# Issue order of the score products: a full key tile's heads 0 and 2 ahead of the half tile's heads 1 and 3

## The chip, the cores and the metric

The kernel runs on one core of one Trainium2 chip. A core has five engines with instruction queues of their own: TensorE (matrix products), VectorE, ScalarE, GpSimd and SyncE (here it issues most DMAs). They meet only through semaphores. TensorE writes its results to PSUM, which has eight banks of 128 partitions; the other data stands in SBUF. The metric is device time in microseconds, the median of several executions.

## The reference

The input x is 4 images of 256 channels, 64 x 64 pixels, in float32. Two attention layers follow each other, each behind a group normalization with 32 groups and with a residual:

```python
x = x + L0(gn(x))      # 8 heads of 32; q from 4096 pixels, k and v by a 2x2 convolution with stride 2
x = x + L1(gn(x))      # 8 heads of 32; attention within 4 areas of 1024 pixels

# L0
attn = softmax((q . (k + pos)) * hd ** -0.5);  out = attn . v
# L1
attn = softmax((q . k) * hd ** -0.5)
out = conv1x1(attn . v + depthwise_conv7x7(v), w_proj, b_proj)
```

In both layers every query meets 1024 keys, so the inner work is the same: for each image, head and query 1024 scores, their exponentials, the sum of these, and the sum of values weighted by them.

## The kernel before, in words

The eight blocks (two layers, four images) are cut into 16 units each: a chunk of 512 queries with one group of four heads (four heads of 32 channels fill the 128 partitions of q and k). A unit goes through its 1024 keys in 8 key tiles of 128, so there are 1024 steps in all, each a unit's key tile. A step's scores are 128 keys (partitions) by 4 heads x 512 queries: four PSUM banks.

PSUM has six banks for scores, as three pairs s0, s1 and s2, and two for everything else. So a step and a half are worked on at a time. A phase (one round of the main loop from L1157, PHASES = 683 in all) computes the scores of one full step and of one half of another step (256 of the 512 queries): three steps in two phases. This is `scores(f)` (L430). Its pair `a` takes heads 0 and 2 of the full step, `b` heads 1 and 3, and `c` the half step's four heads: bank `h // 2` of c, in the right half of the bank for heads 1 and 3, in the left half for heads 0 and 2. The pairs rotate:

```python
a, b, c = [ps_banks(n, "s") for n in ((0, 1, 2) if f % 2 == 0 else (0, 2, 1))]
```

so a stands where the last phase's a stood, c where its b stood, b where its c stood.

A product (`score_product`, L419) is taken for one head at a time, as two matmuls of 64 keys each: the keys' 32 channels are the stationary operand, the queries the moving one. Head h stands on partitions 32h to 32h+31 and so uses the array's rows 32h to 32h+31; the two matmuls of a head use the two halves of its columns. Products of different heads can thus run in the array side by side, but heads 1 and 3 of the half tile and heads 0 and 2 of the half tile write the same two banks of c. A semaphore keeps these apart: each of the half tile's four matmuls for heads 1 and 3 adds one to `in_bank`, and the first matmul for heads 0 and 2 waits for the count (`wait_op`, L454; the Tile framework is told of it with a fence, L455, and adds no semaphore of its own to the counting matmuls, L448).

Three exponentials on ScalarE empty the pairs, in the order a, b, c (`exp_full` L457 with its ACTIVATE on L464, `exp_half` L466 with L475). In a phase, TensorE is given, one after the other: the scores; what the planner puts in of side work (projections, convolution by banded matrices, normalization's statistics, the softmax sums of L508), none to four parts; and the weighted sums of values of the phase before (`weighted`, L479, matmuls on L489). VectorE adds up the exponentials (`add_up`, L494, L499). When a unit ends, its sums go through `divisors` and `divide` (L501, L513), partly by DMA.

Within the main loop the order of every engine is the order in which the program issues (`manual_schedule`, L1100). How much side work goes into a phase is decided while the program is built, by `supply`, `pressure` and `busy` (L214, L248, L279) from counts and due times; they don't look at the order within `scores`.

Of the kernel before, what the change touches and what calls it, by code (L numbers as in the profile page):

```python
# [60 lines left out]
def direct_path(  # L61
# [107 lines left out]
    def ps_banks(n, name):  # L169
        return psum.tile([P, 2, CH], FP, tag=f"s{n}", name=name, bufs=1)  # L170
# [232 lines left out]
    def acc_of(g):  # L403
        if g not in accs:
            accs[g] = pool.tile([P, 4, CH], FP, tag="acc", name="acc", bufs=2)
        return accs[g]

    def pair_of(h):
        return slice(2 * (h % 2), 2 * (h % 2) + 2)

    def acc_half(g, u):
        return acc_of(g).rearrange("p (l b) (u n) -> p u b l n", l=2, u=2)[:, u]

    def parts_of(f):

        full, half = (3 * f + 1) // 2, (3 * f // 2 + 1, 0) if f % 2 == 0 else (3 * f // 2, 1)
        return (full if full < last else None), (half if half[0] < last else None)

    def score_product(out, s, h, cols):  # L419
        g, j = divmod(s, NKT)  # L420
        rows, unit = slice(HD * h, HD * h + HD), units[g]
        return [
            T.matmul(  # L423
                out[n : n + WIDE], lhsT=unit[2]()[rows, unit[0], j * P + n : j * P + n + WIDE],
                rhs=unit[1]()[rows, cols], start=True, stop=True,
            )
            for n in range(0, P, WIDE)
        ]

    def scores(f):  # L430

        full, half = parts_of(f)
        a, b, c = [ps_banks(n, "s") for n in ((0, 1, 2) if f % 2 == 0 else (0, 2, 1))]
        every = slice(0, CH)

        def half_product(h):

            u = half[1]
            return score_product(
                c[:, h // 2, HC * (h % 2) : HC * (h % 2) + HC], half[0], h, slice(HC * u, HC * u + HC)  # L440
            )

        if half is not None:
            for h in (1, 3):
                for first in half_product(h):
                    first.then_inc(in_bank, 1)
                    tc.add_to_no_dep_group(f"first_{f}", first.ins)
                    tc.no_tile_sem_insts.add(first.ins.name)  # L448
                    bank_count[0] += 1
        for h in (0, 2, 1, 3):  # L450
            score_product((a, b)[h % 2][:, h // 2, :], full, h, every)
        if half is not None:
            second = [product for h in (0, 2) for product in half_product(h)]
            second[0].wait_op(in_bank, bank_count[0], "sem-ge")  # L454
            tc.declare_fence(second[0].ins, group=f"first_{f}")  # L455

        def exp_full(n):  # L457
            g, j = divmod(full, NKT)
            if j == 0:
                p = acc_of(g)[:, pair_of(n), :]  # L460
            else:
                p = pool.tile([P, 2, CH], FP, tag="p", name="p", bufs=PB)
            made_p[full, n] = p
            S.activation(p, (a, b)[n], AF.Exp, scale=SCALE)  # L464

        def exp_half():  # L466
            if half is None:
                return
            (g, j), u = divmod(half[0], NKT), half[1]
            if j == 0:  # L470
                p = acc_half(g, u)
            else:
                p = pool.tile([P, 2, CH], FP, tag="p", name="p", bufs=PB).rearrange("p b (l n) -> p b l n", l=2)
            made_p[half[0], 2 + u] = p
            S.activation(p, c.rearrange("p b (l n) -> p b l n", l=2), AF.Exp, scale=SCALE)  # L475

        return [lambda: exp_full(0), lambda: exp_full(1), exp_half]
# [679 lines left out]
    while f < PHASES or before or plan or side or quick or norms_left or to_add or to_divide:  # L1157
        now[0], phase[0] = step, f
        exps = scores(f) if f < PHASES else [lambda: None] * 3
        mine = []  # L1160
        if f < PHASES:
            full, half = parts_of(f)
# [667 lines left out]
```

## Time and profile before

| | |
|---|---|
| median of three runs | 3091.56 us (3090.89 to 3096.43) |
| the profiled execution | 3092.91 us, its span 3090.8 us |
| granted TensorE clock, mean | 0.996 |
| TensorE matmuls busy | 3036.6 us (98% of the span), 47254 instructions |
| TensorE weight loads busy | 1282.2 us (41%) |
| VectorE busy | 2516.2 us (81%) |
| ScalarE busy | 2455.2 us (79%) |
| GpSimd busy | 483.1 us (16%) |
| score matmuls (L423) | 10928 + 10912 matmuls, 543.5 + 537.8 us busy |
| weighted sums (L489, all forms) | 4784 + 4776 matmuls with p, 449.9 + 450.6 us busy |
| exponentials (L464, full tile) | 1194 + 172, 1025 and 1023 ns each |
| exponentials (L475, half tile) | 598 + 84, 1036 and 1045 ns each |

A group of instructions has a line, an engine, an operation, and the tiles that it writes and reads (out<-in). PE stands for TensorE's matmuls, PEld for its weight loads, ACT for ScalarE, DVE for VectorE, POOL for GpSimd, SPq for the queue of SyncE. A float32 matmul of the program stands in the trace as two weight loads and two matmuls, its two passes. A matmul's start is recorded; its end is modelled, and overlapping matmuls are merged in a busy time, so a TensorE that is busy 98% of the time may still stall between matmuls. In a timeline, a row begins with its start and its length in us, merges like instructions, and has in brackets how long the engine sat idle before it and what ended that wait. A row of the waits has who waited for whom, the total in us, how many times, and the longest.

### The profile page before, as it was taken

What the parts mean: (1) busy time and instruction counts of PE and PEld (TensorE: products, weight loads), DVE (VectorE), ACT (ScalarE), POOL (GpSimd) and SP (SyncE); (2) the same over time, 40 slices, a digit from 0 to 9 for tenths busy, and PEclk for the clock granted to TensorE, in tenths of its full rate; (3) what the DMA queues carried; (4) which work ended last, traced back from release to release, by engine and by line L of the source; (5) the groups of instructions that cost most, each with busy time, mean ns of one, the idle gap of its engine ahead of it and who ended that gap; (6) DMA issues with size and microseconds to landing.
All of it is one profiled execution on the core that took longest, in us unless ns stands there. A gap on an engine that the chain in (4) does not pass through costs nothing. (4 is left out here: it accounts for less than half of the span.)

```text
span 3090.8 us, 108514 instructions
## 1 busy us (share of the span) xinstructions
PE 3036.6 (98%) x47254; PEld 1282.2 (41%) x47254; DVE 2516.2 (81%) x2721; ACT 2455.2 (79%) x2988; POOL 483.1 (16%) x921
## 2 busy tenths in 40 slices
PE   9999999999999999999999999999999999999998
PEld 6444333444444444334444444443444444443332
DVE  3788977789887787777888888777888888888888
ACT  3888877888888888788888887777777787788885
POOL 0111111111211111111112111111111111111111
PEclk9999999999999999999999999999999999999999
DMA  5244433566334556777865667667655565542222
GB/s 189 60 100 116 98 80 76 112 147 155 92 99 135 143 151 143 183 184 197 207 171 149 162 172 196 165 170 181 174 153 144 150 163 148 150 106 75 54 68 65
DMA packets 648316, 423.61 MB, mean 137 GB/s; under 512 B 411772, under 2 KB 556636, under 8 KB 647832
## 3 DMA queue, kind: packets, MB, share of 16 engines
q1 hardware_dynamic: 619384, 380.11, 48.6%
q0 software_dynamic: 28448, 36.48, 4.7%
q8 instruction: 373, 6.11, 0.8%
q14 instruction: 111, 0.91, 0.1%
HBM read 318.32 MB, written 98.09 MB: 135 GB/s over the span
## 5 line engine op out<-in xcount | busy, mean ns | idle before, releaser
L499 DVE TENSOR_TENSOR acc<-acc,p 128x1024 f32<-128x1024 f32 x1790 | 2113.9, 1218 | 424.9 <-PE av L489 313.6
L464 ACT ACTIVATE p<-s 128x1024 f32<-128x1024 f32 x1194 | 1159.4, 1025 | 416.5 <-PE s L423 406.0
L475 ACT ACTIVATE p<-s 128x1024 f32<-128x1024 f32 x598 | 619.6, 1036 | 0.3 <-DVE acc L499 0.2
L423 PE MATMUL s<-q,k_A 32*64 32x256 f32 (+1 forms) x10928 | 543.5, 497 | 17.1 <-ACT p L464 16.2
L423 PE MATMUL s<-q,k_B 32*64 32x512 f32 (+1 forms) x10912 | 537.8, 494 | 2.8 <-ACT p L464 2.0
L489 PE MATMUL av<-p,v_B 128*32 128x512 f32 (+1 forms) x4776 | 450.6, 487 | 0.0
L489 PE MATMUL av<-p,v_A 128*32 128x256 f32 (+1 forms) x4784 | 449.9, 486 | 0.0
L423 PEld LDWEIGHTS s<-q,k_A 32*64 32x64 f32 x10928 | 266.3, 131 | 342.6 <-ACT p L464 73.3
L423 PEld LDWEIGHTS s<-q,k_B 32*64 32x64 f32 x10912 | 267.2, 130 | 325.6 <-PE s L423 60.8
L534 POOL DMA_DIRECT2D rb<-recs x508 | 252.0, 502 | 526.7 <-DMA recs<-few 441.1
L532 POOL DMA_DIRECT2D recs<-few x127 | 70.0, 551 | 1407.6 <-DVE sums L531 1248.3
L489 PEld LDWEIGHTS av<-p,v_B 128*32 128x32 f32 x4776 | 149.3, 110 | 264.1 <-issue 238.2
L489 PEld LDWEIGHTS av<-p,v_A 128*32 128x32 f32 x4784 | 149.0, 110 | 228.9 <-issue 187.2
L464 ACT ACTIVATE acc<-s 128x1024 f32<-128x1024 f32 x172 | 167.0, 1023 | 82.1 <-PE s L423 81.9
L508 PE MATMUL den<-acc,ones 128*32 128x512 f32 x1024 | 140.8, 608 | 5.1 <-DVE acc L499 4.3
L524 POOL DMA_DIRECT2D few<-rows x127 | 71.2, 561 | 458.0 <-DMA rows<-den_sb 452.9
L167 PE MATMUL ops<-cv,wp_sb 128*32 128x512 f32 x1024 | 125.1, 598 | 6.1 <-DVE xm L828 3.2
L167 PE MATMUL k1ps<-h,wqkv_sb 128*32 128x512 f32 x1024 | 123.8, 598 | 2.7 <-ACT k_B L730 2.0
L167 PE MATMUL q0ps<-hq,wq_sb 128*32 128x512 f32 x1024 | 124.0, 598 | 1.4 <-ACT q L661 1.4
L167 PE MATMUL q1ps<-h,wqkv_sb 128*32 128x512 f32 x1024 | 124.3, 598 | 0.0
L167 PE MATMUL vals_ps<-hv,wqkv_sb 128*32 128x512 f32 x1024 | 124.1, 598 | 0.0
L167 PE MATMUL v0ps<-wkv,taps 128*32 128x256 f32 x2048 | 124.0, 386 | 0.0
(103 smaller groups left out, 2150.3 us busy)
## 6 DMA issues: line engine op xcount, KB each, us to landing
rows<-vals SPq DMA_DIRECT2D x384, 195.9 KB
rb<-recs POOLq DMA_DIRECT2D x508, 64.0 KB, 3.3
share<-vals SPq DMA_DIRECT2D x128, 195.9 KB
vala<-vout SPq DMA_DIRECT2D x128, 144.0 KB
vals<-vout SPq DMA_DIRECT2D x128, 144.0 KB
vc<-vala SPq DMA_DIRECT2D x64, 288.0 KB
band<-mats SPq DMA_DIRECT2D x96, 176.0 KB
hq<-in_x SPq DMA_DIRECT2D x32, 512.0 KB
```

The source lines that it names most:

```text
L167: T.matmul(out[cols, :], lhsT=lhsT[:, cols], rhs=rhs, start=start, stop=stop)
L423: T.matmul(out[n : n + WIDE], lhsT=unit[2]()[rows, unit[0], j * P + n : j * P + n + WIDE], rhs=unit[1]()[rows, cols], start=True, stop=True,)
L464: S.activation(p, (a, b)[n], AF.Exp, scale=SCALE)
L475: S.activation(p, c.rearrange("p b (l n) -> p b l n", l=2), AF.Exp, scale=SCALE)
L489: T.matmul(out, lhsT=v[:, j, unit[0] * P + HD * h : unit[0] * P + HD * h + HD], rhs=rhs, start=(j == 0 and not u), stop=(j == NKT - 1), sk ...
L499: V.tensor_add(to, to, p)
L508: T.matmul(dens[g][HD * h : HD * h + HD, :], lhsT=ones, rhs=p(h), start=(n == 0), stop=(n == len(sets) - 1),)
L524: G.dma_start(few[:, 0, :], rows.rearrange("h (q n) -> (h q) n", n=CH // HD))
L532: G.dma_start(recs.rearrange("h (q n) -> (h q) n", n=CH // HD), few[:, 1, :])
L534: G.dma_start(rb[HD * h : HD * h + HD, :], recs[h : h + 1, :].to_broadcast([HD, CH]))
```

## The change

In `scores`, the four matmuls of the full tile's heads 0 and 2 (pair a) are issued ahead of the four of the half tile's heads 1 and 3 (pair c). The full tile's heads 1 and 3 (pair b) and the half tile's heads 0 and 2 (pair c) follow as before. The number of instructions, their shapes, the banks, the counts on `in_bank` and the wait for them are the same.

```diff
@@ -440,6 +440,8 @@
                 c[:, h // 2, HC * (h % 2) : HC * (h % 2) + HC], half[0], h, slice(HC * u, HC * u + HC)
             )
 
+        for h in (0, 2):
+            score_product(a[:, h // 2, :], full, h, every)
         if half is not None:
             for h in (1, 3):
                 for first in half_product(h):
@@ -447,8 +449,8 @@
                     tc.add_to_no_dep_group(f"first_{f}", first.ins)
                     tc.no_tile_sem_insts.add(first.ins.name)
                     bank_count[0] += 1
-        for h in (0, 2, 1, 3):
-            score_product((a, b)[h % 2][:, h // 2, :], full, h, every)
+        for h in (1, 3):
+            score_product(b[:, h // 2, :], full, h, every)
         if half is not None:
             second = [product for h in (0, 2) for product in half_product(h)]
             second[0].wait_op(in_bank, bank_count[0], "sem-ge")
```

## The prediction

> **Names.** A phase is one call of scores(f). Its sixteen score products come in four groups of four (two heads, two 64-key column tiles each): H, the half tile's heads 1 and 3 (256 wide, array rows 32-63 and 96-127); A, the full tile's heads 0 and 2 (512 wide, rows 0-31 and 64-95); B, the full tile's heads 1 and 3 (512, same rows as H); C, the half tile's heads 0 and 2 (256, same rows as A). Before: H, A, B, C. After: A, H, B, C. The trace has two passes (two weight loads and two matmuls) for each product, written H1, H2 and so on.
>
> **What bounds the kernel now.** I read the page first, then all waits, then the timeline of single phases. From the page:
>
> ```profile
> span 3090.8 us, 108514 instructions
> PE 3036.6 (98%) x47254; PEld 1282.2 (41%) x47254; DVE 2516.2 (81%) x2721; ACT 2455.2 (79%) x2988; POOL 483.1 (16%) x921
> ```
>
> TensorE has 98%, VectorE and ScalarE about 80%. A busy TensorE may still be stalled inside, so the waits decide (engine and line, who is waited for: total us, times, longest):
>
> ```profile
> ACT p L464 <- PE s L423: 406.0, 506, 2.8
> ...
> PEld s L423 <- PE s L423: 119.1, 631, 0.2
> ...
> PE s L423 <- ACT p L464: 18.2, 23, 5.9
> ```
>
> ScalarE's exponential waits for TensorE 506 times; TensorE's score matmuls wait for ScalarE 23 times. TensorE is the bound. The middle line is a weight load of scores that waits for scores: the fence on in_bank ahead of C, in 631 phases, 0.19 us each. The timeline of a common phase shows where it lies:
>
> ```profile
> 1507.40 0.64 PEld L423 LDWEIGHTS s<-q,k_A 32*64 32x64 f32 x24 [0.41 <-ACT q L661]
> 1507.40 1.55 PE L423 MATMUL s<-q,k_A 32*64 32x256 f32 x32
> ...
> 1508.23 0.27 PEld L423 LDWEIGHTS s<-q,k_A 32*64 32x64 f32 x8 [0.19 <-PE s L423]
> ...
> 1508.59 1.02 ACT L464 ACTIVATE p<-s 128x1024 f32<-128x1024 f32 x1 [0.58 <-PE s L423]
> 1508.88 0.16 PEld L489 LDWEIGHTS av<-p,v_A 128*32 128x32 f32 x8 [0.38 <-issue]
> 1508.88 0.64 PE L489 MATMUL av<-p,v_A 128*32 128x256 f32 x8
> ```
>
> The last eight weight loads (C) come 0.83 us after the head, the next work 1.48 us after it. Record by record, from the first matmul: H1 0, A1 0.027, H2 0.267, B1 0.483, A2 0.507, B2 0.912, C1 0.936, C2 1.152. A 256-wide pass takes 0.216, a 512-wide one 0.429 (start to start); a first pass after its load costs 0.051 more. Rows of H and B end at 0.932+0.429 = 1.361, rows of A and C at 1.172+0.216 = 1.388; 0.088 later the next work starts, at 1.476. 616 of the 680 phases that can be compared have 1.476 within 0.004: the beat is fixed by the array, and the C load at 0.826 is early enough for its slot at 0.936.
>
> The exceptions are 52 phases in which B's bank is late (it waits for the third exponential of the phase before), as here:
>
> ```profile
> 3057.91 0.24 PEld L423 LDWEIGHTS s<-q,k_B 32*64 32x64 f32 x16 [1.11 <-ACT p L464]
> 3057.91 2.00 PE L423 MATMUL s<-q,k_B 32*64 32x256 f32 x32 [0.20 <-ACT p L464]
> ...
> 3058.82 0.24 PEld L423 LDWEIGHTS s<-q,k_B 32*64 32x64 f32 x16 [0.68 <-ACT p L475]
> ...
> 3059.84 0.16 PEld L489 LDWEIGHTS av<-p,v_B 128*32 128x32 f32 x8 [0.78 <-issue]
> ```
>
> There the next work starts 1.93 us after the head. A fresh group loaded at 0.91 costs the phase 0.46.
>
> **What the Trainium skill says.** "TensorE: Matmul & The Clock Gate", section "The cost: per-tile semaphore tail": matmuls that run side by side complete in program order, and their semaphore increments are serialized, about 26 ns each. The trace's semaphore updates agree on the order and not on the size. In a common phase H's four counts stand at 0.655, 0.698, 0.740 and 0.783 (0.0425 apart), A's update at 1.158, B's at 1.563, C's at 1.656. In the late phase that starts at 2812.505, C's last pass starts at 1.235, before B's last at 1.418, yet C's update comes at 2.142, 0.093 after B's 2.049, just as in the common phase: it is held until the earlier product has been reported. The same page's "The mechanism" has starts in strict order as well; this trace does not (C2 before B2 there). "TensorEngine Tiling (Array Packing)", "Key Properties", has a drain at each change of tiling: 0.092 at the head, 0.088 at the end. Its "Gotcha 1: PSUM Pressure" forbids two row tiles in one bank at once, which is what the fence is for; no run here shows it broken.
>
> **The change, part by part.** All time from the first matmul of the phase.
>
> 1. Removed: the head's wait for the second exponential of the phase before; A needs only the first. 28 phases with late B waited at the head for 7.4 us in all (0.27 each). Added: H has a wait of its own. Satisfied, it costs nothing: phase 5 already has a satisfied wait on the fifth load of its first batch, and the loads stay 7 ns apart. TensorE has 598 more waits of that kind. VectorE, GpSimd and SyncE have the same instruction order, ScalarE too; no DMA moves past anything.
>
> 2. Array time: unchanged. A1 0, A2 0.480, slot of C 0.909; H1 0.027, H2 0.293, B1 0.509, B2 0.938, end 0.958+0.429+0.088 = 1.475 against 1.476. The two row pairs swap roles.
>
> 3. The first exponential: the last phase, which has no half tile, issues its 512-wide group first. Its update is at 1.131 instead of 1.158. In a common phase ScalarE starts 0.027 earlier; it waits for TensorE anyway, so worth nothing.
>
> 4. The fence. H's matmuls now stand behind A in program order, and H carries the counts on in_bank that C waits for. If completion is reported in program order, they cannot come before A's 1.131, though H is through at 0.53. Four counts of 0.0425 each: 1.174 to 1.301; a load follows the fourth by 0.0425 (0.783 to 0.826 before): C1 is loaded at 1.344 instead of 0.826, and its slot of 0.909 is lost. From load to second pass 0.267, last of four 0.020, stream 0.216, drain 0.088: next work at 1.344+0.591 = 1.935. Against 1.476 that is 0.459 us per phase. Rows of A and C idle for 0.44. Behind C in TensorE's queue stand side work and the weighted sums, and nothing hides the gap, since TensorE is the bound: 682 phases have a fence, 682 x 0.459 = 313.0 us. What is late next is the whole following phase; ScalarE, DMA and VectorE gain slack.
>
> 5. Stalls that this absorbs. In the 52 late phases B's lateness (24.0 us beyond the beat) lies beside the new gap: each exponential of the phase before now comes about 0.49 earlier against the beat, so B starts near 0.70 and ends by 1.63, before C's 1.85. Less 24.0, and less the 7.4 of their heads. Some 39 us of other waits (15 at long heads, 9 at the ends of other score blocks, 15 among side work, mostly for DMA or ScalarE) get more time to pass; I take 16 of them as gone, bounds 0 and 39.
>
> Sum against the profiled execution's own 3092.9: 3092.9 + 313.0 - 24.0 - 7.4 - 16 = 3358.5. Its time is 1.35 above the median of the runs, so 3357.
>
> Bounds for the fence: if the four counts cost nothing after 1.131, the load is at 1.174 and the phase loses 0.289, 197 us; with the page's 26 ns each the load is at 1.279, 0.394, 269 us; if A's report and each of H's cost 0.1 more in all, 0.56, 382 us. I take 0.0425, since it is what this very semaphore shows in every phase.
>
> **Rivals.** (i) *Not slower: H's counts are given when H ends.* Then the fourth is at 0.810, C is loaded at 0.853, ready 0.051 later at 0.904, before its slot at 0.909: the beat is as before and 3090 to 3092 comes out. It decides as long as the fourth count comes before about 0.84 (C would become the later row pair after a load at 0.885). For it: the array has H's sums by then. Against it: C's held update in the late phases. (ii) *Faster: the shorter head wait counts.* TensorE starts A 0.27 earlier in the 28 phases, and if B did not stand behind the third exponential, 7.4 us would go: 3084. Against it: B there starts at 0.91 because of that exponential, whatever goes first; it also needs (i). (iii) *Slower with more cover*: order holds, but the counts come faster and all 39 us of other stalls go: 3092.9+269-31.4-39-1.35 = 3290. (iv) *Slower with less cover*: 0.459 stays, nothing but the 31.4 is absorbed, and ordering delays add 0.05: 3092.9+313+34-31.4-1.35 = 3407. Were H's second pass also held behind A2 (strict start order), B would end at about 1.60, still before C: no further cost.
>
> **How the numbers follow.** The held fence (main case with iii and iv) 0.87; (i) 0.09, (ii) 0.04. Main value 3357. The range 3285 to 3420 covers the bounds of the count and the cover and leaves (i) and (ii), 0.13, and a little of the tails out. About 0.2% (6 us) is what a measurement of this kernel tells from no change: faster 0.04, same 0.09, slower 0.87.
>
> **What would show it.** Right: in a common phase the C loads stand about 1.34 after the head, with a wait for score products of about 0.7 instead of 0.19, the next work 1.93 after it, the first exponential 1.15 after it; ScalarE's waits for TensorE grow by some 300 us; TensorE's own waits for exponentials nearly vanish. Wrong: C loads at 0.85 and next work at 1.476 (rival i); or a gap in another place, such as B starting late in common phases.

## The result

The kernel takes 3354.27 us with the change (median of four runs, 3353.35 to 3355.16) and 3091.56 before: a ratio of 1.0848, interval 1.0831 to 1.0865. It is 8.5% slower.

The page of the kernel after, its span and its busy times:

```profile
span 3353.1 us, 108514 instructions
...
PE 3325.8 (99%) x47254; PEld 1258.1 (38%) x47254; DVE 2521.7 (75%) x2721; ACT 2479.0 (74%) x2988; POOL 483.4 (14%) x921
```

TensorE is "busy" for 289 us more with the same 47254 matmuls, and nobody else is busier by more than 25 us. The busy time has grown by stalls inside the score groups, which the merged matmuls cover. The waits show them (engine and line, who is waited for: total us, times, longest; lines behind the change have moved on by two, so the full tile's exponential L464 is now L466):

```profile
ACT p L466 <- PE s L423: 600.5, 558, 3.5
...
PEld s L423 <- PE s L423: 453.2, 678, 0.7
...
ACT acc L466 <- PE s L423: 114.0, 83, 2.2
...
PE s L423 <- ACT p L466: 5.5, 2, 3.3
```

The score loads' wait for score matmuls, which is the fence on in_bank, went from 119.1 us in 631 phases (0.19 each) to 453.2 in 678 (0.67 each). TensorE's own waits for exponentials fell from 18.2 to 5.5. A common phase in the timeline of the kernel after:

```profile
1639.82 0.67 PEld L423 LDWEIGHTS s<-q,k_A 32*64 32x64 f32 x24 [0.41 <-ACT p L477]
1639.82 2.01 PE L423 MATMUL s<-q,k_A 32*64 32x512 f32 x32
...
1640.98 1.94 ACT L466 ACTIVATE p<-s 128x1024 f32<-128x1024 f32 x2 [0.89 <-PE s L423]
1641.16 0.21 PEld L423 LDWEIGHTS s<-q,k_A 32*64 32x64 f32 x8 [0.68 <-PE s L423]
1641.76 0.16 PEld L167 LDWEIGHTS k1ps<-h,wqkv_sb 128*32 128x32 f32 x8 [0.39 <-issue]
1641.76 1.06 PE L167 MATMUL k1ps<-h,wqkv_sb 128*32 128x512 f32 x8
```

The last eight loads (C) come 1.34 us after the head and not 0.83, the next work 1.94 after it and not 1.48 (the phase's beat); the first exponential 1.16 after it (1.18 before). Starts read record by record, from the first matmul: A1 0, H1 0.027, H2 0.293, A2 0.480, B1 0.509, B2 0.938, C1 1.345, C2 1.612, next work 1.936. The semaphore updates, which the trace records though no view lists them: A's at 1.132, H's four counts at 1.174, 1.217, 1.259 and 1.302, B's at 1.590. By the start of its last pass, 0.313, and 0.216 for a pass of its width, H had left the array at 0.53. 671 of 679 phases that can be compared have this beat within 0.005.

The whole span, cut at the score groups (from a group's first matmul to the next other matmul, and from there to the next group): inside the groups 1042.2 us before and 1329.1 after, +286.9; between them 1951.6 and 1928.0, -23.6; ahead of the first and behind the last -0.9. But for rounding, the sum is the spans' difference, 262.3.

### The profile page after: what moved, and what is told of

Same layout as the page of the kernel before. It is cut to its first block, busy times and chain, and to the rows that moved or that the text cites. A ratio compares the mean times of both kernels' runs of the same rounds, so it can differ in the third digit from the quotient of the medians.

```text
span 3353.1 us, 108514 instructions
## 1 busy us (share of the span) xinstructions
PE 3325.8 (99%) x47254; PEld 1258.1 (38%) x47254; DVE 2521.7 (75%) x2721; ACT 2479.0 (74%) x2988; POOL 483.4 (14%) x921
## 5 line engine op out<-in xcount | busy, mean ns | idle before, releaser
L466 ACT ACTIVATE p<-s 128x1024 f32<-128x1024 f32 x1194 | 1158.7, 1022 | 611.8 <-PE s L423 600.5
L423 PE MATMUL s<-q,k_A 32*64 32x512 f32 (+1 forms) x10928 | 690.6, 501 | 6.6 <-ACT p L466 5.5
L423 PE MATMUL s<-q,k_B 32*64 32x512 f32 (+1 forms) x10912 | 686.1, 500 | 0.0
L423 PEld LDWEIGHTS s<-q,k_A 32*64 32x64 f32 x10928 | 252.6, 130 | 496.6 <-PE s L423 226.2
L423 PEld LDWEIGHTS s<-q,k_B 32*64 32x64 f32 x10912 | 251.9, 130 | 492.0 <-PE s L423 227.0
L466 ACT ACTIVATE acc<-s 128x1024 f32<-128x1024 f32 x172 | 166.9, 1022 | 114.1 <-PE s L423 114.0
```

The source lines that it names most:

```text
L423: T.matmul(out[n : n + WIDE], lhsT=unit[2]()[rows, unit[0], j * P + n : j * P + n + WIDE], rhs=unit[1]()[rows, cols], start=True, stop=True,)
```

## Experiments

The theory, called held fence: TensorE reports completions in program order, so H's counts stand behind A's report, C's load behind the counts, and C loses its slot. Its main rival is the array: that the new order of work itself costs, whatever the counts do. The kernel before was measured again beside the experiments: 3093.14 us beside the first four, 3095.3 beside the other three. The ratios below are to these. In the diffs, three dots stand for lines that are not shown.

**One count instead of four, in the changed order.** H's last matmul alone counts. The edit, of the kernel after:

```diff
-                for first in half_product(h):
-                    first.then_inc(in_bank, 1)
+                for n, first in enumerate(half_product(h)):
...
-                    bank_count[0] += 1
+                    if (h, n) == (3, 1):
+                        first.then_inc(in_bank, 1)
+                        bank_count[0] += 1
```

> The changed order (A, H, B, C), but only the last of H's four matmuls counts on in_bank, so C waits for one count and not for four. Held fence (counts are given in program order, so not before A's report at 1.131 us of a phase, and one after the other, 0.0425 apart): three matmuls without a count pass in some 0.016 each, the one count stands at about 1.22, C is loaded at 1.27 and not at 1.345, 0.08 less per phase, 682 phases: about 3300 us (3267 if the matmuls without a count cost nothing). Array rival (it is the new order of work in the array that costs, whatever the counts do): 3354 as with four counts.

Measured: 3306.2 us, ratio 1.0693 (1.0675 to 1.0710). The timeline of a common phase in this run:

```profile
1606.52 0.66 PEld L423 LDWEIGHTS s<-q,k_A 32*64 32x64 f32 x24 [0.41 <-issue]
...
1607.79 0.21 PEld L423 LDWEIGHTS s<-q,k_A 32*64 32x64 f32 x8 [0.60 <-PE s L423]
1608.38 0.16 PEld L492 LDWEIGHTS av<-p,v_A 128*32 128x32 f32 x8 [0.39 <-issue]
```

C is loaded at 1.27, next work at 1.86. The single count stands at 1.224, 0.092 behind A's report. With 0.0425 for itself, as between two counts, that leaves some 0.0167 for each of three matmuls that count nothing. The beat is 0.078 shorter, 682 phases give 53, the medians differ by 48. The array does exactly the same work in the same order, so the array rival's 3354 is out.

**One head ahead.** Half of A goes ahead of H, the other half behind it. The edit, of the kernel after:

```diff
-        for h in (0, 2):
-            score_product(a[:, h // 2, :], full, h, every)
+        score_product(a[:, 0, :], full, 0, every)
         if half is not None:
...
-        for h in (1, 3):
-            score_product(b[:, h // 2, :], full, h, every)
+        for h in (2, 1, 3):
+            score_product((a, b)[h % 2][:, h // 2, :], full, h, every)
```

> Only head 0 of A is issued ahead of H; head 2 of A follows H (A's head 0, H, A's head 2, B, C). Held fence: H's counts still stand behind a 512-wide product, whose report comes at about 1.09 us of the phase; C is loaded at about 1.30: 0.42 us more than before per phase, 3315 to 3345 us. Array rival (the cost grows with the work that goes ahead): half of it, about 3220 us.

Measured: 3319.54 us, 1.0730 (1.0712 to 1.0748). The timeline of a common phase:

```profile
1602.33 0.65 PEld L423 LDWEIGHTS s<-q,k_A 32*64 32x64 f32 x24 [0.41 <-ACT cout L1057]
...
1603.62 0.21 PEld L423 LDWEIGHTS s<-q,k_A 32*64 32x64 f32 x8 [0.63 <-PE s L423]
```

The counts stand at 1.115 to 1.243, C's load at 1.285, next work at 1.877. Half the work moved ahead costs 87% of the whole (226 of 261 us above the kernel before), not half of it: the first count comes only 0.06 us sooner than with both heads ahead, since one 512-wide head ahead of H holds its counts nearly as long as two.

**Half of H behind A, in the order of before.** The edit, of the kernel before:

```diff
         if half is not None:
-            for h in (1, 3):
-                for first in half_product(h):
...
+            counted(1)
-        for h in (0, 2, 1, 3):
-            score_product((a, b)[h % 2][:, h // 2, :], full, h, every)
+        for h in (0, 2):
+            score_product(a[:, h // 2, :], full, h, every)
+        if half is not None:
+            counted(3)
+        for h in (1, 3):
+            score_product(b[:, h // 2, :], full, h, every)
```

(`counted(h)` holds the loop over `half_product(h)` with its counts.)

> The order of before, but H's head 3 is issued behind A (H's head 1, A, H's head 3, B, C). Two of the four counts stand ahead of A, two behind it. Held fence: the last two counts come after A's report at 1.14 to 1.16, C is loaded at about 1.27 to 1.29: 0.39 us per phase, 3300 to 3325 us. A rival in which a group is held only by the first matmuls of the queue (H's head 1 goes first again, so the head of the phase is as before): 3091 us.

Measured: 3312.26 us, 1.0708 (1.0690 to 1.0726). The timeline of a common phase:

```profile
1604.34 0.67 PEld L423 LDWEIGHTS s<-q,k_A 32*64 32x64 f32 x24 [0.84 <-ACT q L667]
...
1605.62 0.21 PEld L423 LDWEIGHTS s<-q,k_A 32*64 32x64 f32 x8 [0.61 <-PE s L423]
...
1606.21 0.16 PEld L167 LDWEIGHTS q0ps<-hq,wq_sb 128*32 128x32 f32 x8 [0.39 <-issue]
```

This is the clearest sight of the order in which completions are told: the two counts of head 1 stand at 0.655 and 0.697, as before; A's update at 1.145; the two of head 3 at 1.187 and 1.230, although head 3's second pass starts at 0.31, soon after head 1's at 0.27, and is as short. C is loaded at 1.27. Up to B2, which begins at 0.911, every pass starts within 0.03 us of its time in the kernel before; only C is late.

**The added wait alone, in the order of before.** The edit, of the kernel before:

```diff
         for h in (0, 2, 1, 3):
-            score_product((a, b)[h % 2][:, h // 2, :], full, h, every)
+            made = score_product((a, b)[h % 2][:, h // 2, :], full, h, every)
+            if half is not None and h == 0 and bank_count[0] > 4:
+                made[0].wait_op(in_bank, bank_count[0] - 4, "sem-ge")
```

> The order of before (H, A, B, C); A's first matmul gets a wait of its own, on a value of in_bank that was reached in the phase before, so that it is always met. This is the added wait of the change alone: as many as the change adds, and at a place in the first batch of loads. Held fence: nothing, 3091 us within 5. Rival (a wait in the middle of the batch stops TensorE's queue): 0.05 us or more per phase, 3125 us or more.

Measured: 3093.15 us against 3093.14, ratio 0.9998 (0.9989 to 1.0007). The fence is where it was, as its timeline shows (C's loads 0.82 after the head):

```profile
1606.38 0.64 PEld L423 LDWEIGHTS s<-q,k_B 32*64 32x64 f32 x24 [0.41 <-issue]
...
1607.20 0.27 PEld L423 LDWEIGHTS s<-q,k_B 32*64 32x64 f32 x8 [0.19 <-PE s L423]
```

The run adds 681 waits. That is more than the change itself adds: 597, by the weight loads that wait for ScalarE (1920 in the trace before, 2517 after); and they are on another semaphore. All are met when they are reached, and together they cost nothing beyond the interval, some 3 us.

**The fence taken away, in both orders.** H writes where B overwrites it, so C shares no bank with H. The edit, of the kernel after for A first and of the kernel before for H first:

```diff
-                c[:, h // 2, HC * (h % 2) : HC * (h % 2) + HC], half[0], h, slice(HC * u, HC * u + HC)
+                (c, b)[h % 2][:, h // 2, HC * (h % 2) : HC * (h % 2) + HC], half[0], h, slice(HC * u, HC * u + HC)
...
-                    first.then_inc(in_bank, 1)
...
-            second[0].wait_op(in_bank, bank_count[0], "sem-ge")
...
-            S.activation(p, c.rearrange("p b (l n) -> p b l n", l=2), AF.Exp, scale=SCALE)
+            S.activation(p, c[:, :, :HC].unsqueeze(2).to_broadcast([P, 2, 2, HC]), AF.Exp, scale=SCALE)
```

With A first:

> The changed order (A, H, B, C), without a fence: H writes its sums into B's banks, where B then overwrites them, so C shares no bank with H and waits for no count. What is left out: H's sums reach nobody, and the half tile's exponential reads the heads 0 and 2 twice. H now waits for the third exponential of the phase before (B's banks), which comes up to 0.33 us late in some 250 phases. Held fence: the beat of a common phase is back at 1.476 us, and only late third exponentials cost: 3090 to 3200 us, and within 40 us of the kernel without fence that issues H first. Array rival: some 260 us above that kernel, 3350 us or more.

With H first:

> The control of the run without fence: the order of before (H, A, B, C), H into B's banks, no count, the same exponential. The whole phase now waits at its head for the third exponential of the phase before. Held fence and array rival: the same, 3090 to 3200 us; what it costs above 3091 is the later bank, not the order.

Measured: A first 3139.78 us (1.0153, 1.0136 to 1.0170), H first 3172.82 us (1.0263, 1.0246 to 1.0281). The changed order without its fence, a common phase:

```profile
1603.83 0.67 PEld L423 LDWEIGHTS s<-q,k_B 32*64 32x64 f32 x28 [0.41 <-issue]
1603.83 1.54 PE L423 MATMUL s<-q,k_B 32*64 32x512 f32 x32
...
1604.74 0.15 PEld L423 LDWEIGHTS s<-q,k_B 32*64 32x64 f32 x4 [0.25 <-issue]
...
1605.30 0.16 PEld L486 LDWEIGHTS av<-p,v_A 128*32 128x32 f32 x8 [0.41 <-issue]
```

C's first loads are among the 28 of the first batch, which end within 0.67 us; the second pass's four loads come at 0.91, next work at 1.47. C1 starts at 0.909, ahead of B2 at 0.938: the slot that the prediction gave it. So the changed order has the beat of before, in 449 of 679 phases within 0.001 us, and the array rival, which wanted 3350 or more, is out for good. What both cost above 3095 is B's later bank: the waits of the run with H first have

```profile
PEld s L423 <- ACT p L470: 329.1, 329, 5.8
...
PE s L423 <- ACT p L470: 94.7, 243, 5.3
```

where L470 is the half tile's exponential. The loads' 329.1 us are not all lost, as work issued earlier still runs in the array for a part of each wait; the second line is the time in which no matmul ran. Counted against the common gap ahead of a head, 265 phases with H first lose 129 us at their heads. With A first the same lateness is 93 us inside 214 phases, since A runs while H waits; in 211 of them H starts late. With the few other waits of score groups that makes 134 and 100 us, against 54 in the kernel before: 80 and 46 more, and the medians are 78 and 44 above 3095. Here, where H waits for the third exponential, going ahead with A is worth 33 us. That is the good that one might see in the change; in the kernel before, the head waits that the prediction took as removed are 7.4 us in all.

**One count, in the order of before.** The edit of the first run, on the kernel before.

> The order of before (H, A, B, C) with one count by H's last matmul in place of four. C is loaded at about 0.70 to 0.75 us of a phase and not at 0.826, but its slot in the array comes at 0.936 anyway. Held fence: nothing gained, 3091 us within 5: the counts cost only where C's slot waits for them. Rival (each count costs TensorE its own time): 2046 counts fewer at 0.0425 us, 87 us less, 3004 us.

Measured: 3093.04 us against 3095.3, ratio 0.9995 (0.9986 to 1.0004): no difference. The timeline shows the loads of a phase as one run now, since C's come 0.11 us after those ahead of them and not 0.19:

```profile
1603.70 1.09 PEld L423 LDWEIGHTS s<-q,k_B 32*64 32x64 f32 x32 [0.41 <-issue]
1603.70 1.54 PE L423 MATMUL s<-q,k_B 32*64 32x256 f32 x32
```

C still waits for the count: it stands at 0.705 instead of 0.783, C's load at 0.747 instead of 0.825, and C1 starts at 0.936 as ever. The same three counts that cost 48 us behind A cost nothing ahead of it.

## Why the prediction was right

**The bound** was read rightly: TensorE set the time before and does after.

**Part 1, the added waits**: the prediction has 598, the traces 597; they cost nothing, in line with the run with added waits alone.

**Part 2, the array**: the passes start where they were put, A2 0.480, H2 0.293, B1 0.509, B2 0.938, and C1's slot at 0.909 is seen in the run without fence.

**Part 3, the first exponential**: 1.132 against the 1.131 read off the last phase.

**Part 4, the fence**: C's load 1.343 against 1.344, next work 1.936 against 1.935, 682 x 0.460 = 313.7 against 313.0. The two numbers it was made of, the in-order report and 0.0425 for a count, were both in the trace of before, in phases whose B was late and in the counts of every phase.

**Part 5, the cover**: 313.7 less the measured 262.3 makes 51 us absorbed, against 47.4. The late ends of score groups give 26.8 (313.7 less 286.9) and the stretches between them 23.6. The trace shows where: before, 63 phases ran over the beat, by 32.2 us in all, and 32 heads were late, by 22.0; after, 8 phases by 5.1 and 2 heads by 5.7. The guess of 16 for the other waits was the least founded term, and a little low: 51 less 24.0 and 7.4 leaves 20. That the sum came within 3 us of the measured time is luck to that extent: with the bounds of this term, 0 and 39, it would have been 3373 or 3334.

**A miss without weight**: ScalarE's waits for TensorE were to grow by some 300 us; those of the exponentials for score products grew by 227 (600.5 + 114.0 against 406.0 + 81.9). The prediction shows no working for the 300, and with ScalarE's work unchanged it is more than the whole growth of 265 us that the prediction itself gave.

**The rivals**: (i) and (ii) are refuted by the counts' own times after A; (iii)'s faster counts (26 ns each) did not show, they are 42.5 ns behind A too; (iv)'s further delay neither.

No run beat the kernel before; those that put any part of H behind any part of A while C is fenced were slower by 6.9% or more.

## What to carry to other kernels

In every run here a count on a matmul came only after the reports of all matmuls issued before it. So a fence that waits for short work should not have long work issued ahead of that short work, even where the two run side by side in the array. Before moving a group past another, look for who waits on its semaphore and whether the waiter has slack: here 0.06 us of slack (by the prediction's estimate C's load could have come at 0.885 instead of 0.826) met a delay of 0.52. The busy time of TensorE hid this stall, 98% before and 99% after; the weight loads' waits showed it.

## What the hardware showed that was not expected

That reports come in program order, though second passes on different rows of the array start out of it, the prediction had read off the kernel before. The runs show how far it goes. With A first, H's last pass starts at 0.313, ahead of A's last at 0.500, yet H's counts come behind A's report. Without the fence C is through at 1.361 (its last pass starts at 1.145), before B's last pass ends (0.958 + 0.429 = 1.387), but its update comes at 1.682, 0.092 behind B's 1.590. Reports have prices of their own: 0.0425 us for a matmul with a count, some 0.017 for one without. The hold is not peculiar to the counts on in_bank: with one head of A ahead, A's own update waits for H's counts and comes at 1.302 instead of 1.132, though A's last pass starts only 0.03 later than with both heads ahead (0.527 and 0.500).
